# Second 3x3 convolution of five of sixteen images by pairs of output rows with minimal filtering, and its quantising in 16-bit steps

## The chip, the cores and the metric

The kernel runs on one core of one Trainium2 chip. The metric is the device time of one execution in microseconds (us). One core has five engines with a queue of instructions each: TensorE (PE in the profile; PEld is its weight load), VectorE (DVE), ScalarE (ACT), GpSimd (POOL) and SyncE (SP, which here only starts DMAs). Each engine works through its own queue in order; semaphores tie the queues together.

## What is computed

Sixteen images of 128 channels and 32 x 32 pixels go through two layers. The first is attention with four heads over the 1024 pixels of an image, with a residual. The second, which the change touches, is a pair of quantised 3x3 convolutions:

```python
def act_quant(x):                       # 4 bits: 0 .. 15
    xc = jnp.clip(x, 0.0, 1.0)
    return jnp.round(xc * 15) / 15

identity = x
out = conv3x3(act_quant(x), weight_quant(w1))     # 128 -> 128 channels, padding 1
out = batchnorm(out, gamma1, beta1)               # over images and pixels
out = conv3x3(act_quant(out), weight_quant(w2))
out = batchnorm(out, gamma2, beta2)
return out + identity
```

`weight_quant` rounds to whole numbers from -7 to 7 times one scale per convolution. The kernel convolves the whole numbers (0 to 15 and -7 to 7, exact in bf16, summed exactly in f32 PSUM) and lets the batch norms absorb the scales.

## The kernel before

Channels lie on the 128 partitions throughout. Everything is in `fast_path`; a second path in the file runs only if a flag says that a softmax sum left its range, and it is not taken here.

The attention of the sixteen images is one long software pipeline, `scores` (L487), exponentials (L500), `attend` (L511), softmax sums on VectorE (L520, L522). In its gaps the first convolution of images 0 to 14 is done by two-dimensional minimal filtering, with row sums of the padded image on VectorE (L704, tiles of 128x544 in bf16). The weights of both convolutions are quantised on the way; GpSimd takes the maximum over the partitions (`partition_all_reduce`, L1042). VectorE's L681 scales transformed bf16 weights. At the start GpSimd clears three padded bf16 images (`pads`, 34 x 34, L236) and makes a unit matrix (masks.py).

At the seam, the last head of image 15 is normalised in three cuts. For each, L646 and L647 multiply and add, and `quantize` (L244 or L246, then L247 and L248) scales, clips and rounds in f32 and writes whole numbers into a pad. The first convolution of image 15 then runs directly (`conv`, L273: nine matmuls into one PSUM tile, one per tap, each over a shifted view of the pad), in groups of 15, 8 and 9 rows; L283 takes statistics from PSUM. `keep_clock` (L755) gives PE sixteen matmuls that nobody reads. `bn_params(0)` (L310 to L324) makes one scale and one bias per channel from the mean and variance of all images.

The last part is the second convolution, L836 to L864. `res` tiles are loaded from DRAM for the final residual (L844). For each image: quantise its `ys[b]` into `pads[b % 3]` (L246 on ScalarE, L247 and L248 on VectorE), two images ahead; convolve it in two halves of 16 rows, nine matmuls of 512 columns each (image 0 and image 15 in three groups); copy each PSUM tile to `ys[b]` on ScalarE (L284); take statistics of each half on VectorE (L289). After image 8, `check_sums` (L334 to L351) reduces the softmax sums to the flag: GpSimd takes the maximum over partitions (L350) and VectorE copies it to the flag (L351). After image 15, `bn_params(1)` runs, and L872 to L876 scale, add the residual and write out.

The second convolution of an image is, in the code of before:

```python
for b in range(B):
    rows = starts.get(b, (0, RPH, H))
    for i, (r0, r1) in enumerate(zip(rows, rows[1:])):
        conv(ps_c, "c", b, 1, r0, r1 - r0, group=i if b == B - 1 else None)
    if b + 2 < B:
        quantize(b + 2, ys[b + 2], scale1, bias1)
    if b < B - 1:
        done = statistics(b, 1)
```

The order in each engine's queue is not the order of the source: the tile framework schedules the instructions when the program is built, hands out the buffers of the pools, and sets the semaphores. A tile that takes over the memory of an earlier one waits for its last users.

Of the kernel before, what the change touches and what calls it, by code (L numbers as in the profile page):

```python
# [9 lines left out]
F32 = mybir.dt.float32  # L10
BF16 = mybir.dt.bfloat16
AF = mybir.ActivationFunctionType
ALU = mybir.AluOpType
AX = mybir.AxisListType
PSUM = bass.MemoryType.PSUM

NH = 4
A_LEVELS = 15.0
# [171 lines left out]
def fast_path(  # L190
# [12 lines left out]
    P = 128  # L203
    B, C, N = x.shape
# [4 lines left out]
    W = 32  # L209
    H = N // W  # L210
    NTAP = 9
    RPH = HALF // W
    NPAD = 3
# [18 lines left out]
    ys = [keep.tile([P, N], F32, name=f"y{b}") for b in range(B)]  # L232
    pads = []
    for i in range(NPAD):
        t = padp.tile([P, H + 2, W + 2], BF16, name=f"pad{i}")
# [3 lines left out]
    def quantize(b, src, scale, bias, r0=0, r1=H):  # L239

        cut = slice(r0 * W, r1 * W)
        t = qtp.tile([P, (r1 - r0) * W], F32, tag="qt", name="qt")
        if b == B - 1 and scale == A_LEVELS and r1 == H:
            nc.vector.tensor_scalar(t, src[:, cut], scale, 0.0, ALU.mult, ALU.max)  # L244
        else:
            nc.scalar.activation(t, src[:, cut], AF.Relu, bias=bias, scale=scale)  # L246
        nc.vector.tensor_scalar(t, t, A_LEVELS, MAGIC, ALU.min, ALU.add)  # L247
        return nc.vector.tensor_scalar(  # L248
            pads[b % NPAD][:, r0 + 1 : r1 + 1, 1 : W + 1],
            t.rearrange("p (h w) -> p h w", w=W),  # L250
            MAGIC,
            None,
            ALU.subtract,
        )

    def place(n, b, i):
        if b < B - 1:
            return early[n][:, b * NHF + i, :]
        k = 3 + i * STATS
        return late[n][:, k : k + STATS]  # L260

    def gather(n):
        nc.vector.bn_aggr(late[n][:, 1:3], early[n].rearrange("p g s -> p (g s)"))
        nc.vector.tensor_scalar(
            late[n][:, 2:3], late[n][:, 2:3], float((B - 1) * N), None, ALU.mult
        )

    def conv(pool, tag, b, n, r, rows=RPH, group=None, after=None):

        ps = pool.tile([P, rows, W], F32, tag=tag, name=f"psc{n}_{b}_{r}")  # L270
        for tap in range(NTAP):
            dy, dx = divmod(tap, 3)
            last = nc.tensor.matmul(  # L273
                ps,
                lhsT=wq[n][:, tap, :],
                rhs=pads[b % NPAD][:, r + dy : r + dy + rows, dx : dx + W],
                start=(tap == 0),
                stop=(tap == NTAP - 1),
            )
        ps = ps.rearrange("p h w -> p (h w)")  # L280
        if group is not None:
            with tc.issue_after(after) if after else nullcontext():
                nc.vector.bn_stats(place(n, b, group), ps)  # L283
        nc.scalar.copy(ys[b][:, r * W : (r + rows) * W], ps)  # L284
        return last

    def statistics(b, n):
        for hf in range(NHF):
            last = nc.vector.bn_stats(place(n, b, hf), ys[b][:, ts(hf, HALF)])  # L289
        return last  # L290


    gs = keep.tile([P, 2], F32, name="gs")
    be = keep.tile([P, 2], F32, name="be")
    eps = keep.tile([P, 1], F32, name="eps")
# [3 lines left out]
    def bn_constants():  # L299
        for n, mult in enumerate((A_LEVELS, 1.0)):  # L300
            gamma, beta = bnp_sb[:, 2 * n : 2 * n + 1], bnp_sb[:, 2 * n + 1 : 2 * n + 2]
            nc.vector.tensor_scalar(gs[:, n : n + 1], gamma, sc[n], mult, ALU.mult, ALU.mult)
            nc.vector.tensor_scalar(be[:, n : n + 1], beta, mult, None, ALU.mult)
            nc.vector.tensor_tensor(ss[:, n : n + 1], sc[n], sc[n], ALU.mult)

    def bn_params(n):

        new = lambda what: keep.tile([P, 1], F32, name=f"{what}{n}")
        mv = keep.tile([P, 2], F32, name=f"mv{n}")
        nc.vector.bn_aggr(mv, late[n])  # L310
        mean, var = mv[:, 0:1], mv[:, 1:2]
        rt = new("rt")
        nc.scalar.activation(rt, var, AF.Sqrt, bias=eps, scale=ss[:, n : n + 1])
        v = new("v")
        nc.vector.tensor_scalar(v, var, ss[:, n : n + 1], BN_EPS, ALU.mult, ALU.add)
        r = new("r")
        nc.vector.reciprocal(r, rt)

        t = new("t")
        nc.vector.tensor_scalar(t, r, r, v, ALU.mult, ALU.mult)  # L320
        nc.vector.tensor_scalar(t, t, -0.5, 1.5, ALU.mult, ALU.add)
        scale, bias = new("scale"), new("bias")
        nc.vector.tensor_scalar(scale, r, t, gs[:, n : n + 1], ALU.mult, ALU.mult)
        nc.vector.scalar_tensor_tensor(  # L324
            bias, mean, scale, be[:, n : n + 1], ALU.mult, ALU.subtract, reverse1=True
        )
        return scale, bias
# [9 lines left out]
    def check_sums():  # L337

        sums_range(B - 1)
        ok = keep.tile([P, 2], F32, name="ok")  # L340
        low, high = keep.tile([P, 1], F32, name="low"), keep.tile([P, 1], F32, name="high")
        nc.vector.tensor_reduce(low, ext[:, 0, :], AX.X, ALU.min)
        nc.vector.tensor_reduce(high, ext[:, 1, :], AX.X, ALU.max)
        nc.vector.tensor_scalar(ok[:, 0:1], low, 1.0 / SUM_LIMIT, None, ALU.is_ge)
        nc.vector.tensor_scalar(ok[:, 1:2], high, SUM_LIMIT, None, ALU.is_le)
        bad = keep.tile([P, 1], F32, name="bad")
        nc.vector.tensor_tensor(bad, ok[:, 0:1], ok[:, 1:2], ALU.mult)
        nc.vector.tensor_scalar(bad, bad, -1.0, 1.0, ALU.mult, ALU.add)
        worst = keep.tile([P, 1], F32, name="worst")
        nc.gpsimd.partition_all_reduce(worst, bad, P, bass_isa.ReduceOp.max)  # L350
        nc.vector.tensor_copy(flag, worst[0:1, :])  # L351

    with ExitStack() as ph:
        pool = lambda name, bufs, **kw: ph.enter_context(tc.tile_pool(name=name, bufs=bufs, **kw))
# [29 lines left out]
        for hf in range(NHF):  # L384
            for i, queue in enumerate((nc.sync, nc.scalar)):
                half = (ts(i, P // 2), ts(hf, HALF))
# [285 lines left out]
        D = W // 2  # L672
# [16 lines left out]
        rows, tiles = {}, {}  # L689
# [118 lines left out]
        while step < n_steps or later:  # L808
            if step < n_steps:
                g, j = divmod(step, NCH)  # L810
                b, h = heads[g]
# [24 lines left out]
    with ExitStack() as ph:  # L836
        pool = lambda name, bufs, **kw: ph.enter_context(tc.tile_pool(name=name, bufs=bufs, **kw))
        resp = pool("res", 1)
        ps_c = pool("ps_c", 6, space=PSUM)
        scale1, bias1 = bn_params(0)  # L840
        x1 = []
        for b in range(B):
            t = resp.tile([P, N], F32, name=f"res{b}")
            nc.sync.dma_start(out=t, in_=x1d[b])  # L844
            x1.append(t)

        for r0, r1 in ((0, 10), (10, RPH + 2), (RPH + 2, H)):
            quantize(0, ys[0], scale1, bias1, r0, r1)
        quantize(1, ys[1], scale1, bias1)
        starts = {0: (0, 8, RPH, H), B - 1: (0, RPH, H - 8, H)}  # L850
        for b in range(B):
            rows = starts.get(b, (0, RPH, H))
            for i, (r0, r1) in enumerate(zip(rows, rows[1:])):
                conv(ps_c, "c", b, 1, r0, r1 - r0, group=i if b == B - 1 else None)
            if b + 2 < B:
                quantize(b + 2, ys[b + 2], scale1, bias1)
            if b < B - 1:
                done = statistics(b, 1)
            if b == B // 2:
                with tc.issue_after(done.ins):  # L860
                    check_sums()
            if b == B - 2:
                gather(1)
        scale2, bias2 = bn_params(1)  # L864

        parts = {0: (0, N // 4, N // 2, N), 1: (0, N // 2, N), 2: (0, N // 2, N)}
        for b in range(B):
            ends = parts.get(b, (0, N))
            for lo, hi in zip(ends, ends[1:]):
                y = ys[b][:, lo:hi]  # L870
                if b == 0 and hi <= N // 2:
                    nc.vector.tensor_scalar(y, y, scale2, bias2, ALU.mult, ALU.add)  # L872
                else:
                    nc.scalar.activation(y, y, AF.Identity, bias=bias2, scale=scale2)  # L874
                nc.vector.tensor_tensor(y, y, x1[b][:, lo:hi], ALU.add)  # L875
                nc.sync.dma_start(out=out[b][:, lo:hi], in_=y)  # L876
# [108 lines left out]
def attention_then_quantized_convs(  # L985
# [48 lines left out]
    def conv_weights(n, wp, behind):  # L1034
# [19 lines left out]

    flag = const.tile([1, 1], mybir.dt.int32, name="flag")
    fast_path(
        nc, tc, x, wqk, wvo, bo, bnp, x1d, out, bo_sb, bnp_sb, quad, wq, sc, flag, conv_weights,
        constants,
# [81 lines left out]
```

## Time and profile before

| what | us |
|---|---|
| median of 4 runs | 2117.67 (2117.6 to 2117.81) |
| the profiled execution: its own time | 2117.44 |
| the profiled execution: span from first to last instruction | 2115.6 |
| PE busy | 2084.1 |
| DVE busy | 1454.6 |
| ACT busy | 736.5 |
| POOL busy | 6.9 |
| mean granted TensorE clock, of 1 | 0.994 |

The span is what the profile's times count in; 1.84 us of the execution's own time lie outside it. "Busy" adds up the durations of an engine's instructions. In a timeline row the columns are start (us from the span's start), duration, engine, line, operation, output and input tiles with their sizes (partitions x elements), how many instructions the row merges, and in brackets how long the engine had been idle and what ended that. DVE and ACT instructions overlap their neighbours by some hundredths of a microsecond, so that a row of 0.69 that follows another takes about 0.62 from start to start.

### The profile page before, as it was taken

How to read it: one execution, taken by the hardware profiler on the slowest of the kernel's cores; microseconds unless marked ns; L12 is line 12 of the kernel's file. 1: busy time of each engine (PE TensorE's matmuls, PEld its weight loads, DVE VectorE, ACT ScalarE, POOL GpSimd, SP SyncE). 2: the span in 40 equal slices, each digit the busy share in tenths (PEclk: the TensorE clock that was granted, in tenths of full speed). 3: DMA queues.
4: the chain of work that ended last, by engine and by line, in shares of the span. 5: the costliest groups of instructions: out<-in, count | busy, mean ns of one | idle time of the engine just before them, and what ended most of it. 6: DMA issues, size and time to landing. Idle time of an engine off the chain costs nothing.

```text
span 2115.6 us, 14861 instructions
## 1 busy us (share of the span) xinstructions
PE 2084.1 (99%) x5276; PEld 941.0 (44%) x5277; DVE 1454.6 (69%) x2171; ACT 736.5 (35%) x858; POOL 6.9 (0%) x16
## 2 busy tenths in 40 slices
PE   9999999999999999999999999999999999999994
PEld 4444444444444444444444444444444444444542
DVE  4775667767577676667658666776757667676776
ACT  2233333333333333333333333333333333333365
POOL 0000000000000000000000000000000000000000
PEclk9999999999999999999999999999999999999997
DMA  2000000000000000000000000000000000000044
GB/s 61 12 20 0 0 20 0 20 0 10 10 0 20 0 20 0 1 20 0 20 1 20 0 0 20 0 20 0 14 7 0 20 0 10 0 0 10 0 170 160
DMA packets 11089, 36.81 MB, mean 17 GB/s; under 512 B 1536, under 2 KB 1920, under 8 KB 11008
## 3 DMA queue, kind: packets, MB, share of 16 engines
q1 hardware_dynamic: 9824, 33.10, 4.3%
q10 hardware_dynamic: 1184, 2.69, 0.4%
q8 instruction: 43, 0.70, 0.1%
q14 instruction: 38, 0.31, 0.0%
HBM read 19.01 MB, written 16.78 MB: 17 GB/s over the span
## 4 chain that ended last, share of the span: by engine, by line
PE 98%; DVE 1%; ACT 0%; DMA 0%; issue 0%; ACTq 0%; DVEq 0%
PE pss L487 42%; PE psa L511 41%; PE psv L466 5%; PE psu L453 5%; PE psc L273 3%; PE psw L720 1%; PE psa L628 1%; DVE y L875 0%; ACT y L874 0%; DMA x<-in_x_dram 0%; DVE es L620 0%; DVEq L1061 0%; PE psr L552 0%; DVE late L283 0%; PE ps_b L425 0%
## 5 line engine op out<-in xcount | busy, mean ns | idle before, releaser
L500 ACT ACTIVATE e<-pss 128x1024 f32<-128x1024 f32 x511 | 523.4, 1024 | 1279.8 <-PE pss L487 1246.1
L487 PE MATMUL pss<-u,x 128*128 128x512 f32 (+1 forms) x2064 | 962.4, 589 | 0.0
L511 PE MATMUL psa<-e,vo 128*128 128x512 f32 x2016 | 947.8, 592 | 0.0
L522 DVE TENSOR_TENSOR es<-es,e 128x1024 f32<-128x1024 f32 x378 | 460.5, 1218 | 291.4 <-ACT e L500 291.3
L487 PEld LDWEIGHTS pss<-u,x 128*128 128x128 f32 x2064 | 392.1, 190 | 487.2 <-issue 471.2
L511 PEld LDWEIGHTS psa<-e,vo 128*128 128x128 f32 x2016 | 378.1, 190 | 452.2 <-issue 451.0
L474 DVE COPY vo<-psv 128x512 f32<-128x512 f32 x128 | 88.2, 690 | 265.0 <-PE psv L466 265.0
L453 PE MATMUL psu<-x,at_sb 128*128 128x512 f32 x256 | 131.0, 593 | 0.7 <-DMA x<-in_x_dram 0.6
L466 PE MATMUL psv<-bt_sb,x 128*128 128x512 f32 x256 | 130.2, 592 | 0.0
L534 DVE TRANSPOSE_TENSOR_REDUCE part<-es 128x32 f32<-128x1024 f32 (+1 forms) x66 | 80.6, 1221 | 2.2
L520 DVE TENSOR_TENSOR es<-e,e 128x1024 f32<-128x1024 f32 x63 | 76.7, 1217 | 6.4 <-ACT e L500 6.4
L570 DVE STREAM_TRANSPOSE rb<-sums 128x1024 f32<-128x1024 f32 (+1 forms) x66 | 79.8, 1209 | 1.3
L453 PEld LDWEIGHTS psu<-x,at_sb 128*128 128x128 f32 x256 | 48.6, 191 | 61.9 <-issue 60.3
L466 PEld LDWEIGHTS psv<-bt_sb,x 128*128 128x128 f32 x256 | 48.6, 190 | 61.2 <-issue 57.9
L711 DVE TENSOR_TENSOR tiles<-rows 128x1024 bf16<-128x1024 bf16 x60 | 71.8, 1218 | 1.1 <-PE psw L720 0.6
L458 DVE TENSOR_SCALAR u<-psu,au_sb 128x512 f32<-128x512 f32 x64 | 47.6, 744 | 33.9 <-PE psu L453 33.9
L273 PE MATMUL psc<-pad,wq 128*128 128x512 bf16 (+3 forms) x333 | 67.8, 365 | 0.6 <-DVE pad L248 0.6
L727 ACT COPY wino<-psw 128x512 f32<-128x512 f32 x120 | 64.1, 591 | 0.0
L581 DVE TENSOR_TENSOR av<-av,rb 128x1024 f32<-128x1024 f32 x47 | 57.3, 1220 | 0.4
L582 DVE TENSOR_TENSOR acc<-acc,av 128x1024 f32<-128x1024 f32 x47 | 57.1, 1215 | 0.0
L273 PEld LDWEIGHTS <-wq 128*128 128x128 bf16 x333 | 32.2, 97 | 36.4 <-PE unread L755 1.1
L527 ACT COPY av<-psa 128x512 f32<-128x512 f32 x63 | 36.9, 586 | 29.8 <-PE psa L511 29.8
(121 smaller groups left out, 747.2 us busy)
## 6 DMA issues: line engine op xcount, KB each, us to landing
x_dram<-x SPq DMA_DIRECT2D x16, 512.0 KB, 2.6
res<-x_dram SPq DMA_DIRECT2D x16, 512.0 KB, 9.4
x<-in_x_dram SPq DMA_DIRECT2D x14, 512.0 KB, 3.5
out_dram<-y SPq DMA_DIRECT2D x13, 512.0 KB, 4.1
out_dram<-y SPq DMA_DIRECT2D x5, 256.0 KB, 2.3
raw<-in_cw_dram ACTq DMA_DIRECT2D x2, 576.0 KB, 3.7
x<-in_x_dram ACTq DMA_DIRECT2D x1, 512.0 KB, 3.5
wqk_sb<-in_wqk_dram ACTq DMA_DIRECT2D x1, 385.5 KB, 3.7
```

The source lines that it names most:

```text
L273: last = nc.tensor.matmul(ps, lhsT=wq[n][:, tap, :], rhs=pads[b % NPAD][:, r + dy : r + dy + rows, dx : dx + W], start=(tap == 0), stop=(t ...
L453: nc.tensor.matmul(ps, lhsT=at_sb[:, h, :], rhs=xt[b][:, ts(hf, HALF)], start=True, stop=True)
L466: nc.tensor.matmul(ps, lhsT=xt[b][:, ts(j, P)], rhs=bt_sb.rearrange("p h o -> p (h o)"), start=True, stop=True,)
L474: nc.vector.tensor_copy(vos[b, j], ps)
L487: last = nc.tensor.matmul(ps[:, ts(m, N // len(parts))], lhsT=xt[b][:, ts(key, P)], rhs=us[g][:, queries], start=True, stop=True,)
L500: exps[:] = [nc.scalar.activation(e, ps, AF.Exp).ins]
L511: nc.tensor.matmul(psa[g][m], lhsT=vos[b, j][:, ts(h, P)], rhs=e[:, ts(m, HALF)], start=(j == 0), stop=(j == NCH - 1),)
L520: nc.vector.tensor_tensor(es[g], es.pop((g, 0)), es.pop((g, 1)), ALU.add)
L522: added = nc.vector.tensor_tensor(es[g], es[g], es.pop((g, j)), ALU.add)
L534: nc.vector.tensor_reduce(part, total.rearrange("p (k c) -> p k c", c=Q), AX.X, ALU.add, apply_transpose=True,)
L570: nc.vector.transpose(rb, rinv.unsqueeze(2).to_broadcast([P, n, Q]))
L711: nc.vector.tensor_tensor(tiles[b][:, l % 2], pick(x), pick(y), op)
```

## The change

Images 4, 6, 8, 10 and 12 (`FILTERED`) get their second convolution by pairs of output rows. For output rows 2i and 2i + 1, four row combinations of the padded input (rows d0 to d3 from 2i on) are made: d0 - d2, d1 + d2, d2 - d1, d1 - d3. Each is convolved along the row with three taps: with the upper tap row, with the sum of all three tap rows, with upper minus middle plus lower, and with the lower. That makes four products m0 to m3 with three matmuls of 512 columns each, 12 for an image, in place of 18. The two output rows are m0 + (m1 + m2)/2 and (m1 - m2)/2 - m3. The products are issued in the order m1, m2, m0, m3.

- GpSimd makes the summed tap rows (`middle`, lines 855 to 857 of the changed file) and clears two more padded images (`padf`, 862) at the head of this part. It also makes the row combinations 0 and 3 of each filtered image; VectorE makes 1 and 2 (all on line 895).
- After the four products, ScalarE halves m1 (915) and VectorE does four combinations (916 to 919), of which the second and fourth write `ys[b]`.
- All second-convolution quantising is new (`quantize2`): ScalarE scales, adds the bias, which now includes 128, and writes bf16 (876), where numbers from 128 to 255 are whole, so that the write rounds. VectorE clips to 128 to 143 (879) and subtracts 128 into the pad (880), on 16-bit tiles. Filtered images are quantised four images ahead, the others two.
- The PSUM pool has eight buffers of a bank for six. Filtered images take four, others two.
- In the built program GpSimd's queue reloads its code twice more: ahead of line 855 and ahead of the reduce of `check_sums` (353 in the changed file, whose flag copy is 354).

```diff
+    STEP = 128.0
...
-            nc.vector.tensor_scalar(be[:, n : n + 1], beta, mult, None, ALU.mult)
+            shift = STEP if n == 0 else 0.0
+            nc.vector.tensor_scalar(be[:, n : n + 1], beta, mult, shift, ALU.mult, ALU.add)
...
-        ps_c = pool("ps_c", 6, space=PSUM)
+        steps = pool("steps", 3)
+        padf = pool("padf", 1)
+        rowp = pool("rows", 2)
+        sump = pool("sum", 2)
+        ps_c = pool("ps_c", 8, space=PSUM)
+        FILTERED = (4, 6, 8, 10, 12)
+        D = H // 2
+        middle = padf.tile([P, 2, 3, P], BF16, name="middle")
+        taps = wq[1].rearrange("p (y x) o -> p y x o", x=3)
+        nc.gpsimd.tensor_tensor(middle[:, 1], taps[:, 0], taps[:, 2], ALU.add)
+        nc.gpsimd.tensor_tensor(middle[:, 0], middle[:, 1], taps[:, 1], ALU.add)
+        nc.gpsimd.tensor_tensor(middle[:, 1], middle[:, 1], taps[:, 1], ALU.subtract)
+        weights = (taps[:, 0], middle[:, 0], middle[:, 1], taps[:, 2])
+        filtered_pads = []
+        for i in range(2):
+            t = padf.tile([P, H + 2, W + 2], BF16, name=f"padf{i}")
+            nc.gpsimd.memset(t, 0.0)
+            filtered_pads.append(t)
...
+        def quantize2(b, r0=0, r1=H):
+            pad = filtered_pads[FILTERED.index(b) % 2] if b in FILTERED else pads[b % NPAD]
+            t = steps.tile([P, (r1 - r0) * W], BF16, tag="steps", name="steps")
+            nc.scalar.activation(
+                t, ys[b][:, r0 * W : r1 * W], AF.Identity, bias=bias1, scale=scale1
+            )
+            nc.vector.tensor_scalar(t, t, STEP, STEP + A_LEVELS, ALU.max, ALU.min)
+            nc.vector.tensor_scalar(
+                pad[:, r0 + 1 : r1 + 1, 1 : W + 1],
+                t.rearrange("p (h w) -> p h w", w=W),
+                STEP,
+                None,
+                ALU.subtract,
+            )
+            if b not in FILTERED:
+                return
+            rows[b] = rowp.tile([P, 4, D, W + 2], BF16, tag="rows", name=f"rows2_{b}")
+            pick = lambda r: pad[:, r : r + 2 * D - 1 : 2, :]
+            four = ((0, 2, ALU.subtract), (1, 2, ALU.add), (2, 1, ALU.subtract), (1, 3, ALU.subtract))
+            for k in (1, 2, 0, 3):
+                x, y, op = four[k]
+                engine = nc.vector if k in (1, 2) else nc.gpsimd
+                engine.tensor_tensor(rows[b][:, k], pick(x), pick(y), op)
...
+        def filtered_conv(b):
+            m = [None] * 4
+            for k in (1, 2, 0, 3):
+                m[k] = ps_c.tile([P, D, W], F32, tag="c", name=f"psf_{b}_{k}")
+                for dx in range(3):
+                    nc.tensor.matmul(
+                        m[k],
+                        lhsT=weights[k][:, dx, :],
+                        rhs=rows[b][:, k, :, dx : dx + W],
+                        start=(dx == 0),
+                        stop=(dx == 2),
+                    )
+            y = ys[b].rearrange("p (i r w) -> p r i w", r=2, w=W)
+            new = lambda what: sump.tile([P, D, W], F32, tag=what, name=f"{what}_{b}")
+            half, total = new("half"), new("total")
+            nc.scalar.mul(half, m[1], 0.5)
+            nc.vector.scalar_tensor_tensor(total, m[2], 0.5, half, ALU.mult, ALU.add)
+            nc.vector.tensor_tensor(y[:, 0], m[0], total, ALU.add)
+            nc.vector.scalar_tensor_tensor(half, m[2], -0.5, half, ALU.mult, ALU.add)
+            nc.vector.tensor_tensor(y[:, 1], half, m[3], ALU.subtract)
...
-            rows = starts.get(b, (0, RPH, H))
-            for i, (r0, r1) in enumerate(zip(rows, rows[1:])):
-                conv(ps_c, "c", b, 1, r0, r1 - r0, group=i if b == B - 1 else None)
-            if b + 2 < B:
-                quantize(b + 2, ys[b + 2], scale1, bias1)
+            if b in FILTERED:
+                filtered_conv(b)
+            else:
+                ends = starts.get(b, (0, RPH, H))
+                for i, (r0, r1) in enumerate(zip(ends, ends[1:])):
+                    conv(ps_c, "c", b, 1, r0, r1 - r0, group=i if b == B - 1 else None)
+            if b + 2 < B and b + 2 not in FILTERED:
+                quantize2(b + 2)
+            if b + 4 in FILTERED:
+                quantize2(b + 4)
```

More of the change, by code (lines that the diff above doesn't have):

```diff
@@ new lines, in fast_path @@
+        rows = {}
+        def filtered_conv(b):
[18 more added lines that the diff above has]
+            nc.vector.tensor_tensor(y[:, 1], half, m[3], ALU.subtract)
@@ L847, in fast_path @@
         for r0, r1 in ((0, 10), (10, RPH + 2), (RPH + 2, H)):
-            quantize(0, ys[0], scale1, bias1, r0, r1)
-        quantize(1, ys[1], scale1, bias1)
+            quantize2(0, r0, r1)
+        quantize2(1)
         starts = {0: (0, 8, RPH, H), B - 1: (0, RPH, H - 8, H)}
         for b in range(B):
-            rows = starts.get(b, (0, RPH, H))
-            for i, (r0, r1) in enumerate(zip(rows, rows[1:])):
-                conv(ps_c, "c", b, 1, r0, r1 - r0, group=i if b == B - 1 else None)
-            if b + 2 < B:
-                quantize(b + 2, ys[b + 2], scale1, bias1)
+            if b in FILTERED:
[8 more added lines that the diff above has]
+                quantize2(b + 4)
```

## The prediction

> **What bounds the kernel now.** I read the page first, then the busy time by stretches, then the order of time in the last 120 us. The page's busy line and its chain say that TensorE is the whole kernel; the change touches only its last part, line L273 (pss, psa, psv and psu are the attention).
>
> ```profile
> PE 2084.1 (99%) x5276; PEld 941.0 (44%) x5277; DVE 1454.6 (69%) x2171; ACT 736.5 (35%) x858; POOL 6.9 (0%) x16
> PE pss L487 42%; PE psa L511 41%; PE psv L466 5%; PE psu L453 5%; PE psc L273 3%; PE psw L720 1%; PE psa L628 1%; DVE y L875 0%; ACT y L874 0%; DMA x<-in_x_dram 0%; DVE es L620 0%; DVEq L1061 0%; PE psr L552 0%; DVE late L283 0%; PE ps_b L425 0%
> ```
>
> The stretches of the second convolution (columns: stretch, length, busy us of PE, PEld, DVE, ACT, POOL, clock, DMA): PE is busy all of the 20 us at clock 1.00, DVE about 13 of 20, POOL nothing.
>
> ```profile
> 2040.00:2060.00 20.00, 20.00 (x92) 8.81 (x91) 13.49 (x21) 12.23 (x16) 0.00 (x0) 1.00 0.00 0
> 2060.00:2080.00 20.00, 20.00 (x92) 8.81 (x91) 12.37 (x27) 9.25 (x13) 0.35 (x1) 1.00 0.01 2
> ```
>
> In the timeline one image takes 2043.06 - 2039.09 = 3.97 us, which is 18 matmuls of 512 columns: 0.2205 us each. Every evacuation waits for PE (1.34 us), and VectorE's queue stands still for 0.6 us per image.
>
> ```profile
> 2039.09 0.59 ACT L284 COPY y<-psc 128x512 f32<-128x512 f32 x1 [1.34 <-PE psc L273]
> 2039.71 0.69 DVE L289 BATCH_NORM_STATS2 early<-y 128x6 f32<-128x512 f32 x1
> ...
> 2043.06 0.59 ACT L284 COPY y<-psc 128x512 f32<-128x512 f32 x1 [1.34 <-PE psc L273]
> 2043.06 0.70 DVE L248 TENSOR_SCALAR pad<-qt 128x1024 bf16<-128x1024 f32 x1 [0.62 <-PE psc L273]
> ```
>
> Ahead of it is the seam between attention and convolutions, where VectorE is the path: the last third of image 15 is normalised and quantised (L646 to L248), then PE finishes the first convolution and L310 to L324 make the scale.
>
> ```profile
> 2014.76 4.16 PE L273 MATMUL psc<-pad,wq 128*128 128x480 bf16 x27
> 2015.06 0.32 SPq L844 DMA_DIRECT2D res<-x_dram  x1
> 2015.71 0.42 DVE L647 TENSOR_TENSOR x<-x,rb 128x256 f32<-128x256 f32 x1
> 2016.17 0.29 DVE L244 TENSOR_SCALAR qt<-x 128x256 f32<-128x256 f32 x1
> 2016.50 0.29 DVE L247 TENSOR_SCALAR qt<-qt 128x256 f32<-128x256 f32 x1
> 2016.83 0.30 DVE L248 TENSOR_SCALAR pad<-qt 128x256 bf16<-128x256 f32 x1
> ```
>
> **Removed from TensorE.** Five images go from 18 to 12 matmuls of the same width: 30 x 0.2205 = 6.62 us, all on the path. The first pad is ready sooner: two steps on 128x320 cost 0.33 each now (L247 and L248 at 2022), and 16-bit ones by the rows of L681 (128x768 0.359, 128x1024 0.416, so 0.26 for 320) 0.14 us less together. The stage after 2086.7 is moved, not altered. Nothing added to PE: the loads and columns are alike. In sum -6.76 us if all added work is hidden.
>
> **Added beside it.** ScalarE: Identity for Relu, 16 bits for 32 (same 1.24; no row shows the narrow output, and ScalarE has 40% to spare), one scaling of 0.58 in place of two copies of 0.59. The constant in `be`, the eight PSUM buffers: nothing. VectorE, from start to start: both quantising steps 0.35 each (L681) for 0.62; per filtered image four combinations of 512 at 0.62 (as L620 and L289) and two row sums at 0.37 (L704, 0.436 long). GpSimd: ten row differences of 128x544, three weight sums of 128x384, two memsets, and two code reloads.
>
> *GpSimd's prices.* No two-input instruction of it is in the trace. Its rows:
>
> ```profile
> 1.04 3.06 POOL L236 MEMSET pad<- 128x1156 bf16 x3
> ...
> 4.06 0.21 POOL masks.py:197 MEMSET ident<- 128x128 f32 x1
> 11.68 0.28 POOL masks.py:199 TENSOR_SCALAR_AFFINE_SELECT ident<-ident 128x128 f32<-128x128 f32 x1 [7.41 <-issue]
> 55.01 1.24 POOL L1042 PARTITION_ALL_REDUCE alpha<-pmax  x1 [43.04 <-DVE pmax L1040]
> 86.57 1.24 POOL L1042 PARTITION_ALL_REDUCE alpha<-pmax  x1 [30.33 <-DVE pmax L1040]
> 2062.45 0.35 POOL L350 PARTITION_ALL_REDUCE worst<-bad  x1 [1974.63 <-DVE bad L348]
> ```
>
> The memsets (0.21 for 128 elements, 1.06 for 1156) give 0.10 + 0.00083 n; the select reads one operand as well and takes 0.07 more on 128, 0.57 ns an element. With two operands: 0.10 + 0.00197 n, so 1.17 us for 544 and 0.86 for 384. Bounds: the memset's price (0.55 and 0.42) and three times its slope (1.5 and 1.06).
>
> *Do VectorE and GpSimd wait for each other?* The same reduce took 1.24, 1.24 and 0.35 us. Beside the long ones VectorE had just begun a sum of two SBUF operands (below; the other ran from 86.39 to 87.61); both reduces end 0.2 us after it. Beside the short one ran L289, with one operand. So GpSimd waited for such a VectorE instruction to end.
>
> ```profile
> 54.79 1.22 DVE L520 TENSOR_TENSOR es<-e,e 128x1024 f32<-128x1024 f32 x1
> ```
>
> The other direction is not in the trace; I take it to be alike, for sums of two SBUF operands, and for SBUF tensor_scalars, which run at twice the rate of sums (L247 0.69 for 1024, L522 1.22) and so need a second way too. The Trainium skill says so of both ("SBUF — State Buffer", Who interferes with whom): whichever starts first keeps the shared pair for its whole instruction. By that rule the sum is the one below; without it, -6.76 stands.
>
> *The seam.* In the built order the weight sums and memsets are GpSimd's first work there, released by PE's last attention matmul, as is the first res load: 2015.0. Taking turns: sum 2015.0 to 2015.86, L647 2015.88 to 2016.30, memset to 2016.92, L244 to 2017.23, sum to 2018.09, L247 to 2018.40, memset to 2019.46, L248 to 2019.78 in place of 2017.13. PE is free for the last third at 2014.76 + (480 + 256) x 9 / 512 x 0.2205 = 2017.6, so 0.5 us is slack: +2.15 us on the path. If memsets don't block, +0.6; if GpSimd's whole chain (4.7 us) goes first, L248 ends at 2020.7 and it is +3.05.
>
> *The convolutions.* Count from PE's start on image 4. Image 10's fourth product needs the PSUM bank that image 8's third combination (L918) frees; PE gets there at 3 x (2.65 + 3.97) + 1.98 = 21.8 us. VectorE's order from the first row sum of image 8 (released at 2.85, by image 4's last product) to that L918 has 27 instructions: 10 combinations and 8 statistics at 0.62, 4 row sums at 0.37, 3 pad writes and 2 clamps at 0.35: 14.4 us, done at 17.2, 4.6 us early. For image 12 another 7.7 us (with the sum check's eight small ones, 1.3) stand against 6.6 of PE: 3.5 left. In that stretch GpSimd has 6 differences, 7.0 us. What they block of VectorE lies between none and all: 0 or 7.0 - 3.5 = 3.5 us lost. I take two thirds, since both engines' row work is released by the same product: 4.7 - 3.5 = +1.2.
>
> The pad write starts one element into its row. By the Trainium skill ("VectorE: DVE Perf Modes", 2×_1P) pairs need 4-byte alignment, and it would take 0.70 like L248: 1.1 us more of VectorE by image 12, the sum -2.3 in place of -3.4; the Trainium skill ("Vector Engine (DVE) Microarchitecture Reference", 5.1) also reports that alignment made no difference when measured. No row here shows it; I take 0.35.
>
> *Waits behind waits.* The pad of image 8 waits for GpSimd's rows of image 4, and pads 7 and 5 stand behind it; GpSimd is done by about 2033, image 5 starts at 2041. The flag copy (L354 after) waits for GpSimd's reduce, behind a code reload of 7.4 us (the 7.41 row): ready at 15.9 + 2.4 + 7.4 = 25.7, when VectorE gets there at 24 or later. Behind it stand L919 of image 10 and the statistics; PE needs that L919 at 31.1. So it is hidden unless a reload takes over 12 us.
>
> Sum: -6.76 + 2.15 + 1.2 = **-3.4 us**: the profiled execution's 2117.44 (its span 2115.6, 1.84 around it) becomes 2114.0; the median was 0.23 above that execution, so 2114.3.
>
> **Rivals.** (1) *The port costs nothing* and GpSimd runs beside VectorE: -6.76, 2110.9. For it: the reduce is another kind of instruction. Against: three rows that fit waiting. Chance 0.22. (2) *GpSimd goes first at every tie*, so that VectorE becomes the bound: at 1.17 us a difference 3.05 + 3.5 - 6.76 = -0.2; slower than before from about 1.2 us on; at 1.5 us 3.65 + 5.5 - 6.76 = +2.4, 2120.1; past +4.2 from 1.72 us. For it: its memsets follow each other with no gap (three in 3.06 us), and VectorE had only 6 to 7 us of 20 free before five images got four combinations each. Chance 0.20. (3) *The reload lasts*: twice 7.4 is 3 us over its cover: 2113.9 with (1), 2117.3 with my sum. Against: the one seen took 7.4. Chance 0.06. That PE's work isn't cut can't be: the built program has 12 matmuls for each of the five.
>
> **How the numbers follow.** The forecast has 0.52. About 0.2% (4.2 us) is what a measurement of this kernel can tell from no change. Faster by more: rival 1 and the forecast's cheap end (sums near 0.6 us), 0.33. Slower by more: rival 2's dear end and reloads, 0.15. Between: 0.52. The range reaches from rival 1 to rival 2's dear end, 2110.6 to 2120.6; the forecast's own is 2111.8 to 2116.5.
>
> **What would show it.** L273's 333 matmuls down to 243, beside 60 of the new line; L857's sums on POOL from 2015.0; L244 to L248 stretched or late, ending near 2019.8; POOL differences near 1.2 us with VectorE's row sums and clamps longer beside them; PE waits of about a microsecond ahead of the fourth products of images 10 or 12. It is wrong if the seam ends where it did, if PE idles more than 2 us in the filtered images, or if the flag copy holds VectorE.

## The result, and the profile after

The changed kernel takes 2113.71 us (median of 37 runs, 2112.83 to 2115.28) against 2117.64 us (57 runs of the kernel before beside it): a ratio of 0.9981, 95% interval 0.9976 to 0.9986, 3.9 us less. 2114.3 was forecast. The profiled execution took 2112.86 us, its span 2111.1.

The busy line and the chain by line, of the changed kernel's page:

```profile
PE 2077.8 (98%) x5246; PEld 938.0 (44%) x5247; DVE 1467.5 (70%) x2201; ACT 730.8 (35%) x853; POOL 23.3 (1%) x31
PE pss L490 42%; PE psa L514 41%; PE psv L469 5%; PE psu L456 5%; PE psc L273 2%; PE psw L723 1%; PE psf L904 1%; DVE y L955 1%; PE psa L631 0%; ACT y L954 0%; DMA wvo_sb<-in_wvo_dram 0%; DVE qt L247 0%; ACTq L390 0%; DVE es L623 0%; PE ps_b L428 0%
```

PE has 30 matmuls less and is still the chain; a step of VectorE's seam, L247 (`DVE qt`), is now among the steps listed. The stretches of the second convolution (columns: stretch, length, busy us of PE, PEld, DVE, ACT, POOL, clock, DMA):

```profile
2040.00:2060.00 20.00, 20.00 (x92) 8.84 (x91) 19.55 (x36) 13.35 (x18) 6.83 (x6) 1.00 0.00 0
2060.00:2080.00 20.00, 20.00 (x93) 8.81 (x91) 19.64 (x43) 5.29 (x9) 0.44 (x1) 1.00 0.01 2
```

VectorE went from 13 of 20 us to 19.6, and PE is still busy all the time: no matmul of the filtered images waited. The seam, from the timeline (a merged row bears the shape of its first instruction, so the last row stands for all 81 matmuls up to image 4):

```profile
2014.51 3.03 PE L273 MATMUL psc<-pad,wq 128*128 128x480 bf16 x18
2014.83 0.91 POOL L855 TENSOR_TENSOR middle<-wq 128x384 bf16<-128x384 bf16 x1 [1927.28 <-PE psa L631]
2015.46 0.56 DVE L650 TENSOR_TENSOR x<-x,rb 128x256 f32<-128x256 f32 x1
2015.68 1.06 POOL L862 MEMSET padf<- 128x1156 bf16 x1
2016.06 0.83 DVE L244 TENSOR_SCALAR qt<-x 128x256 f32<-128x256 f32 x1
2016.71 0.94 POOL L856 TENSOR_TENSOR middle<-middle,wq 128x384 bf16<-128x384 bf16 x1
2016.92 1.87 DVE L247 TENSOR_SCALAR qt<-qt 128x256 f32<-128x256 f32 x1
2017.60 1.05 POOL L862 MEMSET padf<- 128x1156 bf16 x1
2018.62 0.94 POOL L857 TENSOR_TENSOR middle<-middle,wq 128x384 bf16<-128x384 bf16 x1
2018.83 0.88 DVE L248 TENSOR_SCALAR pad<-qt 128x256 bf16<-128x256 f32 x1
2019.76 1.28 PE L273 MATMUL psc<-pad,wq 128*128 128x288 bf16 x9 [2.22 <-DVE pad L248]
...
2025.03 16.05 PE L273 MATMUL psc<-pad,wq 128*128 128x256 bf16 x81 [0.53 <-DVE pad L880]
```

L244, L247 and L248 took 0.83, 1.87 and 0.88 us for the 0.3 they took before. Each ends 0.14 to 0.15 us behind the end of a GpSimd instruction (2016.74, 2018.65, 2019.56), and PE waits 2.22 us for the last of them.

To compare kernels without what goes on ahead, the tail of each profiled execution is cut in three: A from PE's first L273 on 128x480 to the second convolution's first matmul, B from there to the end of PE's last matmul, C to the span's end. The second column is where A begins. In the kernel before, the four times are 2014.76, 2023.01, 2086.68 (PE's last row begins at 2085.74 and lasts 0.94) and 2115.6. The last column is the median of all executions.

| kernel | A begins | A | B | C | median |
|---|---|---|---|---|---|
| before | 2014.76 | 8.25 | 63.67 | 28.9 | 2117.64 |
| changed | 2014.51 | 10.52 | 57.06 | 29.0 | 2113.71 |
| preparation early | 2015.19 | 8.14 | 57.06 | 28.9 | 2111.48 |
| memsets early | 2016.27 | 9.07 | 57.06 | 29.0 | 2112.18 |
| sums early | 2014.82 | 8.47 | 57.06 | 29.1 | 2111.62 |
| rows on VectorE | 2017.00 | 10.53 | 57.06 | 28.9 | 2113.77 |
| early, and rows on VectorE | 2014.75 | 8.14 | 57.06 | 29.0 | 2110.83 |
| quantising alone | 2015.14 | 8.14 | 63.67 | 29.0 | 2117.82 |
| six images | 2016.24 | 8.14 | 57.13 | 30.2 | 2111.98 |
| differences twice | 2016.58 | 8.13 | 62.32 | 29.3 | 2116.55 |

Between before and after: B -6.61, A +2.27, together -4.3 us. A begins between 2014.5 and 2017.0 although what precedes it is the same work; that is the run-to-run spread, and it comes from the first microseconds (last section). Medians therefore agree with the table only to some 0.5 us. One execution of the kernel with both edits took 3074.94 us at a granted clock of 0.68, and its ratio below is that of the other five.

### The profile page after: what moved, and what is told of

Same layout as the page of the kernel before. It is cut to its first block, busy times and chain, and to the rows that moved or that the text cites. A ratio compares the mean times of both kernels' runs of the same rounds, so it can differ in the third digit from the quotient of the medians.

```text
span 2111.1 us, 14862 instructions
## 1 busy us (share of the span) xinstructions
PE 2077.8 (98%) x5246; PEld 938.0 (44%) x5247; DVE 1467.5 (70%) x2201; ACT 730.8 (35%) x853; POOL 23.3 (1%) x31
## 4 chain that ended last, share of the span: by engine, by line
PE 98%; DVE 1%; ACT 0%; DMA 0%; issue 0%; ACTq 0%; DVEq 0%
PE pss L490 42%; PE psa L514 41%; PE psv L469 5%; PE psu L456 5%; PE psc L273 2%; PE psw L723 1%; PE psf L904 1%; DVE y L955 1%; PE psa L631 0%; ACT y L954 0%; DMA wvo_sb<-in_wvo_dram 0%; DVE qt L247 0%; ACTq L390 0%; DVE es L623 0%; PE ps_b L428 0%
## 5 line engine op out<-in xcount | busy, mean ns | idle before, releaser
L273 PE MATMUL psc<-pad,wq 128*128 128x512 bf16 (+3 forms) x243 | 49.0, 359 | 2.8 <-DVE pad L248 2.2
L564 DVE COPY side<-part 32x32 f32<-32x32 f32 x252 | 43.0, 170 | 4.7
```

The costliest lines, as they stand in the source:

```text
L273: last = nc.tensor.matmul(ps, lhsT=wq[n][:, tap, :], rhs=pads[b % NPAD][:, r + dy : r + dy + rows, dx : dx + W], start=(tap == 0), stop=(t ...
```

## The experiments

The kernel before was timed beside all of them: its median was 2117.86 beside the first four and 2117.77 beside the next four. The probe at the end was run once.

**Preparation early.** The tile `wino` and the buffer of `tiles` move to a pool that outlives the attention, and the weight sums and memsets are issued into them once image 14 has no more use for them:

```diff
+        def prepare():
+            a = over.tile([P, 2048], BF16, tag="wino", name="prep_a")
+            middle = prep["middle"] = a[:, 0:768].rearrange("p (k x o) -> p k x o", k=2, x=3)
...
+            c = over.tile([P, 2048], BF16, tag="tiles", name="prep_c")
...
+            prep["pads"] = [a[:, 768 : 768 + n], c[:, 0:n]]
+            for i in range(2):
+                nc.gpsimd.memset(prep["pads"][i], 0.0)
...
+        at(end + when[2] + 3, prepare)
```

> The three weight sums and two memsets on GpSimd are issued some 30 us earlier, in the attention of image 15, where PE is the bound; nothing else is changed. Theory A (the seam is late because VectorE's L650 to L248 wait for GpSimd's instructions): L248 ends about 2.3 us earlier against the last attention matmul, PE has no 2.2 us wait for it; 2113.7 - 2.3 = 2111.4 us, and the two groups of times (near 2113.0 and 2114.5) become one, because no order of turns is left to vary. Rival B (the seam is late because of the loads of res that start there, or the change of buffers): 2113.7 us, the 2.2 us wait of PE stays. Rival C (the work is only moved: beside the attention's sums of 1.22 us it holds VectorE and so PE): 2112.5 to 2113.7 us.

Measured: 2111.48 us, ratio to before 0.9970 (0.9959 to 0.9981). The timeline at the seam:

```profile
2016.14 0.42 DVE L651 TENSOR_TENSOR x<-x,rb 128x256 f32<-128x256 f32 x1
2016.60 0.29 DVE L245 TENSOR_SCALAR qt<-x 128x256 f32<-128x256 f32 x1
2016.93 0.29 DVE L248 TENSOR_SCALAR qt<-qt 128x256 f32<-128x256 f32 x1
2017.25 0.30 DVE L249 TENSOR_SCALAR pad<-qt 128x256 bf16<-128x256 f32 x1
```

The steps have their old lengths (lines are one higher), PE's 2.22 us wait is gone, and A is 8.14. Rival B falls: the loads of `res` still start there, 0.30 us behind A's begin as in the changed kernel. So GpSimd's five instructions cost 10.52 - 8.14 = 2.38 us of path. Rival C falls too: PE waits for none of them in the attention. The times did not become one group: five lie from 2111.33 to 2111.49, two at 2112.64 and 2113.02. That part of theory A was wrong; the spread is older than the seam (last section).

**Memsets early, sums at the seam**; the memsets alone are in `prepare`:

```diff
-            nc.gpsimd.memset(t, 0.0)
+                nc.gpsimd.memset(prep["pads"][i], 0.0)
```

> The two memsets alone are issued in the attention of image 15; the three sums stay at the seam, now back to back from 2014.8 to 2017.6. If memsets hold VectorE as sums do (theory A): VectorE gets its last turn behind the third sum, L248 ends near 2018.1 in place of 2019.7: 2112.1 us. If memsets don't hold it (rival: only two-input instructions do), the sums alone set the end as before, at most 0.5 us earlier: 2113.2 to 2113.7 us.

Measured: 2112.18 us, ratio 0.9973 (0.9964 to 0.9983).

```profile
2017.57 0.97 POOL L869 TENSOR_TENSOR middle<-middle,wq 128x384 bf16<-128x384 bf16 x1
2017.81 0.88 DVE L245 TENSOR_SCALAR qt<-x 128x256 f32<-128x256 f32 x1
2018.62 0.91 POOL L870 TENSOR_TENSOR middle<-middle,wq 128x384 bf16<-128x384 bf16 x1
2018.73 0.95 DVE L248 TENSOR_SCALAR qt<-qt 128x256 f32<-128x256 f32 x1
2019.71 0.30 DVE L249 TENSOR_SCALAR pad<-qt 128x256 bf16<-128x256 f32 x1
```

As theory A said: L245 and L248 each end 0.15 us behind a sum of GpSimd's (2018.54 and 2019.53), and the last step runs in its usual 0.30. PE waits 0.76 us, and A is 9.07.

**Sums early, memsets at the seam**, the other half, all three sums moved into `prepare`:

```diff
-        middle = padf.tile([P, 2, 3, P], BF16, name="middle")
-        nc.gpsimd.tensor_tensor(middle[:, 1], taps[:, 0], taps[:, 2], ALU.add)
...
+            middle = prep["middle"] = a[:, 0:768].rearrange("p (k x o) -> p k x o", k=2, x=3)
+            nc.gpsimd.tensor_tensor(middle[:, 1], taps[:, 0], taps[:, 2], ALU.add)
...
```

> The three sums alone are issued in the attention of image 15; the two memsets stay at the seam, 2014.8 to 2016.9. Theory A (memsets hold VectorE): L244 or L247 ends 0.15 behind the second memset and L248 near 2017.5, 0.0 to 0.5 us of PE wait: 2111.5 to 2112.0 us. Rival (memsets hold nothing): L650 0.42, L244, L247 and L248 0.25 each, L248 ends at 2016.8 and PE never waits: 2111.4 us. The lengths of L244 and L247 decide, more than the time.

Measured: 2111.62 us, ratio 0.9972 (0.9962 to 0.9983).

```profile
2015.10 2.06 POOL L871 MEMSET padf<- 128x1156 bf16 x2 [47.93 <-PE psa L632]
...
2015.77 0.42 DVE L651 TENSOR_TENSOR x<-x,rb 128x256 f32<-128x256 f32 x1
2016.23 1.08 DVE L245 TENSOR_SCALAR qt<-x 128x256 f32<-128x256 f32 x1
2017.34 0.29 DVE L248 TENSOR_SCALAR qt<-qt 128x256 f32<-128x256 f32 x1
```

The two memsets run from 2015.10 to 2017.16. The sum L651 passes beside them in its usual 0.42; the scalar step L245 is held until 0.15 us behind them. So memsets hold scalar steps from SBUF to SBUF, and not sums of two SBUF operands. Sums alone cost A 9.07 - 8.14 = 0.93 us, memsets alone 0.33, both 2.38, more than the 1.26 of the two. In the changed kernel's rows L247 is passed over once: it waits for the sum L856, and then for the memset behind it, 1.05 us. That this is the whole surplus is read from the rows; no run changes the order alone.

**All row combinations on VectorE**, the seam as in the changed kernel:

```diff
-                engine = nc.vector if k in (1, 2) else nc.gpsimd
-                engine.tensor_tensor(rows[b][:, k], pick(x), pick(y), op)
+                nc.vector.tensor_tensor(rows[b][:, k], pick(x), pick(y), op)
```

> The ten row differences are VectorE's (0.38 each from start to start, 3.8 us in all) in place of GpSimd's (1.2 each); the seam is as in the changed kernel. Theory A (GpSimd's differences cost VectorE more than they take off it: beside them VectorE's sums took 2.28 for two in place of 0.8, L879 1.15 and L880 1.35 in place of 0.42, some 5 us in all): VectorE's busy time from 2040 to 2080 falls from 39.2 to about 38 us, no PE wait: 2113.7 us, within 0.4. Rival (VectorE, busy 98% of those 40 us, has no room for ten more, and GpSimd's help carries the change): 2 to 4 us of PE waits ahead of the fourth products of images 10 and 12, 2115.5 to 2117.5 us.

Measured: 2113.77 us, ratio 0.9980 (0.9971 to 0.9989), the changed kernel's time. First the changed kernel's VectorE beside GpSimd's differences, then this kernel's four row sums, and last the whole of B in the changed kernel and in this one:

```profile
2030.48 2.41 POOL L895 TENSOR_TENSOR rows<-padf 128x544 bf16<-128x544 bf16 x2 [10.92 <-DVE padf L880]
2030.91 2.28 DVE L895 TENSOR_TENSOR rows<-padf 128x544 bf16<-128x544 bf16 x2
...
2043.81 2.40 POOL L895 TENSOR_TENSOR rows<-padf 128x544 bf16<-128x544 bf16 x2 [6.38 <-PE psf L904]
2044.07 1.15 DVE L879 TENSOR_SCALAR steps<-steps 128x1024 bf16<-128x1024 bf16 x1 [0.45 <-ACT steps L876]
...
2045.14 1.35 DVE L880 TENSOR_SCALAR pad<-steps 128x1024 bf16<-128x1024 bf16 x1
...
2050.42 2.22 POOL L895 TENSOR_TENSOR rows<-padf 128x544 bf16<-128x544 bf16 x2 [4.21 <-PE psf L904]
2050.43 1.86 DVE L289 BATCH_NORM_STATS2 early<-y 128x6 f32<-128x512 f32 x3
```

```profile
2033.41 1.48 DVE L894 TENSOR_TENSOR rows<-padf 128x544 bf16<-128x544 bf16 x4
2025.03:2082.09 57.06, 57.06 (x276) 26.67 (x276) 53.98 (x107) 31.61 (x44) 12.10 (x11) 1.00 0.25 101
2027.53:2084.59 57.06, 57.06 (x276) 26.68 (x276) 51.81 (x117) 32.37 (x44) 0.38 (x1) 1.00 0.25 101
```

Four row sums alone take 1.48 us, two beside GpSimd 2.28; clamp and pad write take 1.15 and 1.35 for 0.42. Statistics (three in 1.86) are not held. Over the five pairs VectorE lost 1.54 + 1.54 + 0.73 + 0.93 + 0.28 + 0.46 = 5.5 us (the last two at L880 near 2052 and L879 near 2058), and GpSimd saved it ten sums of 1.48 / 4, 3.7 us. That is 1.8 us lost by these rows; over the whole of B VectorE is busy 53.98 us with the help and 51.81 without it, 2.2 us less. (From 2040 to 2080, the stretch that was expected to fall to about 38 us, it is 39.19 and 38.01, but this kernel's B begins 2.5 us later, so those 40 us hold different work.) PE waits for nothing in B, and the rival falls.

**Both edits**: the early preparation, and the rows on VectorE.

> Both edits: sums and memsets in the attention of image 15, and all four row combinations on VectorE, so that GpSimd does nothing beside the seam or the second convolution but the flag's reduce. Theory A (all that the change lost was at the seam): as with the early preparation alone, 2111.4 us within 0.4, PE's one wait in the convolutions the 0.5 us behind the keep-clock matmuls; VectorE is ahead by about 4.5 us where PE starts image 10's fourth product (0.15 us with GpSimd's differences). Rival (GpSimd's differences also cost PE something that the waits don't show): 2110.0 to 2110.9 us.

Measured: 2110.83 us, ratio 0.9965 (0.9952 to 0.9978), the fastest here, by 2.9 us against the changed kernel. The median falls in the rival's range, but A, B and C are those of the early preparation (8.14, 57.06, 29.0 for 28.9), so the 0.65 us between the two medians, which come from different groups, is not in the part that differs. That GpSimd's differences cost PE anything is not shown.

**Quantising alone**: `FILTERED = ()`, and none of GpSimd's preparation.

> No image is filtered and nothing is prepared on GpSimd; the quantising in 16-bit steps from 128 stays. Theory A: the seam from PE's first matmul on 128x480 to the second convolution lasts 8.14 us in place of 8.25 (with the early preparation it did) and the 288 matmuls take their 63.5 us: 2117.5 us, within 0.2 of before. Rival (16-bit steps free VectorE, and with it PE, by more than the first pad): 2115.5 to 2117.0 us.

Measured: 2117.82 us, ratio 1.0000 (0.9991 to 1.0009). B is one unbroken row:

```profile
2023.28 63.67 PE L273 MATMUL psc<-pad,wq 128*128 128x256 bf16 x306 [0.53 <-DVE pad L869]
```

A is 0.11 us shorter than before, the first pad's share of 16-bit steps. The rest frees VectorE (22.0 us busy from 2040 to 2080, for 25.9 before), which PE has no use for.

**Six images**: the kernel with both edits, and image 13 filtered too.

```diff
-        FILTERED = (4, 6, 8, 10, 12)
+        FILTERED = (4, 6, 8, 10, 12, 13)
```

> The kernel without GpSimd, with image 13 filtered too, six in all. Theory A (VectorE is at its limit: with five images it has 2.9 us of waits for PE left behind image 12, a sixth takes 4 x 0.60 + 4 x 0.38 = 3.9 us more of it while PE gets 1.3 us shorter): PE ends 1.3 us earlier, VectorE's last statistics come 1 to 2 us behind it; net gain 0 to 0.9 us against five: 2110.6 to 2111.4 us. Rival B (VectorE still has room): the whole 1.32 us, 2110.1 us. Rival C (VectorE's backlog stops PE for banks ahead of the last images): 2111.8 to 2113.5 us.

Measured: 2111.98 us, ratio 0.9972 (0.9961 to 0.9983), slower than five by 1.15 us. That is in rival C's range, with a wait of PE's near the end:

```profile
2076.89 0.41 DVE L890 TENSOR_SCALAR pad<-steps 128x1024 bf16<-128x1024 bf16 x1
...
2077.36 4.15 PE L274 MATMUL psc<-pad,wq 128*128 128x512 bf16 x27 [1.24 <-DVE pad L890]
```

Not a bank, as I had put it, but the pad of image 15 is late: VectorE gets to L890 behind the combinations of images 12 and 13, and PE waits 1.24 of the 1.32 us that it had saved. So B is 57.13 us for 57.06, and the sixth image gains nothing. That it loses is another matter: C is 1.2 us longer. From PE's last matmul to VectorE's last sum it is 22.1 us in both kernels; the difference is in the output's DMAs behind it, whose 512 KB pieces took 4.6 us to land in the median, for 4.0. Why they did is open.

**GpSimd's differences twice**, on the kernel with the early preparation:

```diff
-                engine.tensor_tensor(rows[b][:, k], pick(x), pick(y), op)
+                for _ in range(1 if k in (1, 2) else 2):
+                    engine.tensor_tensor(rows[b][:, k], pick(x), pick(y), op)
```

> Sums and memsets early, and each of GpSimd's ten row differences issued twice; VectorE's own work is unchanged. It prices the sharing in the convolutions. Theory A (each difference holds VectorE's two-operand sums and clamps for most of its 1.15 us, and VectorE was only 0.15 us ahead at image 10's fourth product): PE waits in front of the fourth products of images 10 and 12, 2 to 5 us in all: 2113.5 to 2116.5 us. Rival B (the ten more run beside VectorE's work on PSUM and statistics, which they don't hold): 2111.5 us. Rival C (GpSimd itself becomes late: PE waits for rows, not for banks): 2112 to 2114 us with the waits on rows.

Measured: 2116.55 us, ratio 0.9995 (0.9986 to 1.0004): 5.1 us lost by ten more differences. PE's waits (in total, how many, the longest, in us), and the end of the first one:

```profile
PE psf L915 <- DVE y L928: 2.8, 2, 1.4
PE psc L274 <- DVE pad L890: 2.1, 2, 1.6
...
2051.77 0.68 DVE L928 TENSOR_TENSOR y<-psf,total 128x512 f32<-128x512 f32 x1
2052.51 0.83 PE L915 MATMUL psf<-rows,wq 128*128 128x512 bf16 x3 [1.43 <-DVE y L928]
```

Two waits for PSUM banks, and two for pads (1.6 for image 5's; the other 0.5 is the first pad's, as in every kernel with the new quantising). That is theory A, at the top of its range. Rival C was right that PE can wait for something other than a bank, but it is a pad, written late by VectorE, and not GpSimd's rows. The banks are those of the fourth products of images 6 and 10, not 10 and 12, and they are freed by L928, which is L917 of the changed kernel: PE goes on 0.06 us after its end.

**A probe**: 14 sums and 14 memsets on GpSimd in the attention of image 15. The built queue alternates them.

> The changed kernel with 14 sums of 128x544 in 16 bits and then 14 memsets of 128x1156 added on GpSimd in the attention of image 15 (their results are not read), beside VectorE's sums of two 32-bit operands of 1024 elements (1.22 us alone), its column reductions and its transposes. It shows which kinds wait for each other; its time is not compared. Theory A (sums of two SBUF operands take turns in both directions, memsets hold only VectorE's scalar steps): GpSimd's sums grow from 1.15 to 1.15 to 2.4 us where a VectorE sum runs, VectorE's sums from 1.22 to 1.3 to 2.4 us; beside the memsets both keep their 1.22 and 1.06 us. Rival (only GpSimd waits, VectorE never does for sums): VectorE's sums stay at 1.22 us throughout, as in the profile of before, where a reduce waited for one.

```profile
1980.15 1.22 POOL L777 TENSOR_TENSOR probe_c<-wq 128x544 bf16<-128x544 bf16 x1
1980.40 8.57 DVE L526 TENSOR_TENSOR es<-es,e 128x1024 f32<-128x1024 f32 x4
...
1989.00 1.25 DVE L538 TRANSPOSE_TENSOR_REDUCE part<-es 128x32 f32<-128x1024 f32 x1
1990.28 7.32 DVE L565 COPY side<-part 32x32 f32<-32x32 f32 x4
...
1996.51 1.07 POOL L779 MEMSET probe_a<- 128x1156 bf16 x1
```

VectorE's sums take 2.14 us each (1.22 alone), about the 2.17 us of one sum and one memset of GpSimd's, as they would if each waited for a sum and then ran beside the memset. The column reduction keeps its 1.25. The four small copies, 0.72 us elsewhere in this profile, take 7.32 us: 0.81 for the first and 2.16 for each of the others, and the last ends as GpSimd's last memset does (1997.58). GpSimd's first sums, beside VectorE's, took up to 1.79 us, later ones 1.22, and its memsets 1.06 throughout. So sums wait for sums in both directions, and the rival falls. (PE once waits 7.9 us for VectorE here, which is the probe's price.)

## Why the prediction was right, and where it was not

**Removed from TensorE, -6.62.** B went from 63.67 to 57.06: -6.61. Right. **The first pad, -0.14.** 0.11. Right.

**GpSimd's prices.** 0.91 to 0.94 us for a weight sum (0.86 said), 1.06 for a memset, 1.1 to 1.2 for a difference (1.17). Right within a tenth, from memsets and one select alone.

**The seam, +2.15.** 2.38, shown by taking GpSimd's work away. L248 ends 5.20 us behind A's begin (2019.71 - 2014.51); 5.02 was said (2019.78 - 2014.76). The turns were not as drawn, in two places. The drawing holds GpSimd back twice, for L244 and for L247 (0.31 us each); in the trace its five instructions follow each other from 2014.83 to 2019.56 without a pause. And the drawing has L247 between a sum and the second memset, so that L248 waits for that memset alone; in the trace L247 was passed over there, GpSimd going first at this tie as rival 2 had it, and L248 waited for the third sum behind the memset. The two errors nearly cancel, so the closeness of the number is in part luck.

**The convolutions, +1.2.** Nothing: PE never waited. This is the step that failed: VectorE was held, but mostly ahead of the stretch that the term charges, and PE needed less of it than the term says. Three things were wrong.

- "Two thirds" of the differences: over all ten, 5.5 of 11.7 us were held, since the last two pairs fell beside statistics, which aren't.
- The count began when image 8's first row sum was released, 2.85 us into image 4. VectorE got there at 2047.94, 7.0 us in. With all rows on VectorE it got there 3.9 us in (2047.29, image 4 at 2043.42), so the first three pairs of differences had put it behind: they held it for 4.7 of the 5.5 us and had saved it four sums, 1.5. The 27 instructions then took 14.65 us (14.4 said), of which only 0.7 was waiting for GpSimd.
- The bank: I had it freed by the third combination, L918; it is the second, L917. The combinations of image 10 beside image 12's last two products (L904 here begins with the third; the fourth follows after 3 x 0.2205 us):

```profile
2068.24 0.68 DVE L917 TENSOR_TENSOR y<-psf,total 128x512 f32<-128x512 f32 x1
2068.68 1.49 PE L904 MATMUL psf<-rows,wq 128*128 128x512 bf16 x6
2068.84 0.68 DVE L918 SCALAR_TENSOR_TENSOR half<-psf,half 128x512 f32<-128x512 f32 x1
```

PE began image 12's fourth product at 2068.68 + 3 x 0.2205 = 2069.34, before L918 of image 10 ended (2069.52), and the doubled kernel's waits name L917. That one ended at 2061.99 for image 8 and 2068.92 for image 10, 0.74 and 0.42 us ahead of PE. So the term was not far off: 0.4 us was all that kept it at nothing, and ten more differences turned it into 5.1.

**The pad write at an element's offset.** L880 takes 0.43 us on 1024 elements and the aligned L879 0.43: the 0.35 from start to start that I took. The Trainium skill ("Vector Engine (DVE) Microarchitecture Reference", 5.1), by which alignment makes no difference, agrees with this trace; the 4 bytes asked for in "VectorE: DVE Perf Modes" were not needed here.

**Reload and flag copy.** The reload's two instructions (`MODIFY_POOL_CONFIG`) stand in the trace at 2059.4, right behind GpSimd's last difference (2059.24), and the reduce L353 began at 2068.12, 0.14 us behind its input. The 8.7 us between would hide a reload of 7.4 us, so rival 3 did not occur; how long this one took is not shown. The reload ahead of L855 ran at 87.5 us, with nothing to wait for it.

**The sum.** -6.61 + 2.38 - 0.11 = -4.34 us by the trace; -3.4 was forecast, and the medians differ by 3.93. The 0.9 us between forecast and trace are the convolutions' 1.2 less 0.2 at the seam. **Rival 1**, that the port costs nothing, is refuted by the early preparation: it gained the 2.2 us that the rival says weren't there. **Rival 2**, GpSimd first at every tie and VectorE the bound, is right of one tie at the seam, and VectorE is the bound in the doubled kernel (60.0 us busy of B's 62.32).

The median came 0.6 us from the forecast and the sum by the trace 0.9. Medians agree with the table only to 0.5 us, so the nearer of the two is no merit of the prediction.

## What to carry to other kernels

Before a helper engine is given part of a full engine's work, subtract what its instructions hold: here ten sums lent to GpSimd saved VectorE 3.7 us and cost it 5.5, and five small preparations at the seam cost 2.4 us of a possible 6.6. Preparation belongs where the path is another engine's, even if memory for it must be taken over from a tile that has just died. And an engine that is 98% busy beside a chain that doesn't wait for it is at its limit, not free: by rows, a filtered image costs VectorE 2 x 0.35 + 1.48 + 4 x 0.6 + 2 x 0.6 = 5.8 us, any other 1.9, for the 1.32 that PE saves, and the sixth already gained nothing.

## What the runs showed of the hardware

VectorE and GpSimd take turns by kind of instruction, not by engine. GpSimd's sums hold VectorE's sums of two SBUF operands (1.22 to 2.14 us) and its scalar steps and copies from SBUF to SBUF; its memsets hold the latter (L245 1.08 for 0.29) and not the former (0.42 as ever). Statistics (three in 1.86 us) and the column reduction (1.25) did not wait for sums. The Trainium skill ("SBUF — State Buffer", Who interferes with whom) states this split, and the traces agree with it in each of these numbers. Not expected was who goes next. With a memset queued behind the sum, VectorE's waiting step was passed over at the change from sum to memset and got its turn behind the memset (L247 1.87 us for 0.29, three copies 2.16 each for 0.18). Behind a weight sum with another sum queued it got its turn at once (L245 0.88, in the kernel with the memsets early). Why the two differ is not shown.

The spread between the profiled executions arises in the first 12 us. In all ten kernels of the table A begins 2005.38 or 2005.39 us behind the same matmul near the start (`scores`, right behind the `ps_b` ones), which itself begins between 9.12 and 11.62. PE's first four matmuls of 128x512, in the changed kernel and in the one with rows on VectorE, whose code is the same up to the second convolution:

```profile
4.81 2.11 PE L456 MATMUL psu<-x,at_sb 128*128 128x512 f32 x4 [0.17 <-DVE at_sb L422]
```

```profile
4.82 2.08 PE L456 MATMUL psu<-x,at_sb 128*128 128x512 f32 x2 [0.17 <-DVE at_sb L422]
7.30 2.08 PE L456 MATMUL psu<-x,at_sb 128*128 128x512 f32 x2 [0.40 <-DMA x<-in_x_dram]
```

About 0.5 us each there and 1.0 here, and the 2.5 us by which the second is late at 10 us (11.62 for 9.12) is still there at 2017. The granted clock is 1.00 in both from 4 to 12 us; why the matmuls differ is not shown. A gain of a microsecond is read from the stage, not from two spans.
